# Router logits of three batches, one token tile at a time between the shared expert's matmuls, in a decoder layer

## The chip, the cores and the metric

The kernel runs on one core of one Trainium2 chip, as one program. The metric is the device time of one execution in microseconds (us); a time of the kernel is the median of several runs. One further execution is recorded by the hardware profiler, and all rows of a profile come from it.

A core has five engines that work through queues of their own and wait for each other through semaphores: PE (TensorE, matmuls and transposes), DVE (VectorE), ACT (ScalarE), POOL (GpSimd) and SP (SyncE, which here only issues DMAs). Matmuls write to PSUM[...]; everything else stands in SBUF or in DRAM.

## What is computed

One decoder layer on x of shape (4, 512, 512) in float32, with three parts, each on a layer norm of x and added to it:

```python
x = x + _L0_attn_ref(_layernorm(x), ...)     # a state space layer (conv, gate, scan)
x = x + _L0_xattn_ref(_layernorm(x), ctx_512, ctx_512)   # 32 query heads, 8 key heads of 16
x = x + _L0_ffn_ref(_layernorm(x), ...)      # mixture of experts
```

The last part is where the change lies. With x as 2048 tokens of 512:

```python
router_logits = x @ gate_w                       # 2048 x 16
scores = sigmoid(router_logits)
selected = top_k(scores + expert_bias, 2)
shared = silu(x @ shared_gate_w) * (x @ shared_up_w) @ shared_down_w
routed = sum over the two selected experts of weight * expert(x)
out = shared + routed
```

## The kernel before

Tokens stand 128 to a tile: NT = 16 tiles, TB = 4 tiles to each of B = 4 batches. The residual `res` stays in SBUF.

**Attention as the main loop.** After the state space layer of batch 0, the loop at L732 goes over 32 units (batch, key head) in 8 steps each. A step computes two score matmuls for the maxima of the next unit (`maxima`, pm, L496, with DVE's reduce L502), two for the weights of this unit (`weights`, pw, L513, with ACT's exponential L517), and in every second step `values` (pav, L522). Once a unit there are transposes: ptq and ptm of the queries (L484), ptv of the result (L531, `finish`). pm and pw alternate in the two buffers of the pool `p_sc`, so the pm of a step waits for the reduce of the step before it.

**Filler.** After each step `fill(step)` (L706) issues pieces of other work on PE: first the state space layers of batches 1 to 3, then `beside_last` (L668), the feed forward of batches 0 to 2. Such work is a generator that yields the us that a piece is thought to take; `fill` gives each step a quota, the total of the work over the steps left, and issues pieces until what is owed is paid, so after a long piece some steps get none. DVE and ACT work of the filler is put off by a step or more through `lag`. The orders on PE, DVE and ACT are as written; those of POOL and SP come from a scheduler. When the last filler begins, `open_ffn` (L546) opens its buffers and issues the loads of its weights on SP, fills a tile `zero` on POOL and stores it to the spare rows of h_d and of the output.

**The feed forward of one batch**, as filler:
- `ffn_first` (L587) normalizes the first two token tiles into `hn`, of which there are two buffers (tag "hn"). `zero` is a tile of the same tag.
- `ffn_input` (L591): for each of four tiles it stores hn to the DRAM copy h_d (L609), which the experts gather from later, transposes it (pth, L612), copies it to hT (ACT, L613) and normalizes the tile after next into the buffer set free. After the four tiles it computes the logits: `logits(j)`, four matmuls of 128x16 per tile (L601), one piece per tile, all into one PSUM tile pl, and then one copy to lgt (L622). With a bank_l given, as for batch 3 behind the main loop, the logits alternate with the transposes.
- `ffn_start` (L580) puts the norm statistics of the next batch (bnf, mvf, rstdf) into DVE's lagged work.
- `shared` (L624): for each of two halves f of the hidden size, pg and pu (L632, each four matmuls of 128x512, in two pieces), tanh on ACT (L640), two products on DVE (L643, L649); then pe (L655), one per token tile, added to res (L660) and stored to the output (L662).

In `beside_last` the next batch's statistics are begun after `ffn_input`, and `shared` runs on while they are made. PSUM tiles of all of these (pt.., pth, pl, pg, pu, pe) come from one pool of three banks (`bank`, tag "mm").

Behind the main loop come batch 3's feed forward input, the choice of experts from lgt (L840 on), and the loop over 47 blocks of tokens with gathered expert weights.

Of the kernel before, what the change touches and what calls it, by code (L numbers as in the profile page):

```python
# [10 lines left out]
F32 = mybir.dt.float32  # L11
# [6 lines left out]
P = 128  # L18
B, L, D = 4, 512, 512
NT = B * L // P  # L20
TB = L // P
# [10 lines left out]
E, F = 16, 256  # L32
# [13 lines left out]
def decoder_layer(ctx: ExitStack, tc: tile.TileContext, a: dict, out: bass.AP):  # L46
    nc = tc.nc
# [61 lines left out]
    def bank(name, shape=(P, L)):  # L109
        return p_mm.tile(list(shape), F32, tag="mm", name=name)  # L110
# [44 lines left out]
    def until(*tests):  # L155

        while not all(t() for t in tests):
            yield None
# [385 lines left out]
    ffn = {}  # L544

    def open_ffn():  # L546
        ssm_pools.close()
        hp_ = ctx.enter_context(tc.tile_pool(name="ffn_h", bufs=1, side="right"))
        ffn["hp"] = hp_
        ffn["hT"] = hp_.tile([P, DC, NT * P], F32, name="hT")  # L550
        ffn["lgt"] = hp_.tile([P, NT, E], F32, name="lgt")
        gw = ffn["gw"] = hp_.tile([P, DC, E], F32, name="gw")
        nc.sync.dma_start(out=gw, in_=a["gate_w"].rearrange("(c p) e -> p c e", p=P))
        ebias = ffn["ebias"] = hp_.tile([P, E], F32, name="ebias")
        nc.sync.dma_start(out=ebias, in_=a["expert_bias"].partition_broadcast(P))
        gu = ffn["gu"] = hp_.tile([P, DC, 2 * F], F32, name="gus")
        nc.sync.dma_start(
            out=gu[:, :, 0:F], in_=a["shared_gate_w"].rearrange("(c p) f -> p c f", p=P)
        )
        nc.sync.dma_start(  # L560
            out=gu[:, :, F:], in_=a["shared_up_w"].rearrange("(c p) f -> p c f", p=P)
        )
        zero = hp_.tile([P, D], F32, tag="hn", bufs=2, name="zero")
        nc.gpsimd.memset(zero, 0.0)
        for rows in (h_d, out):
            nc.sync.dma_start(out=rows[ts(NT, P), :], in_=zero)
        dn = ffn["dn"] = hp_.tile([P, FC, D], F32, name="dns")
        nc.sync.dma_start(out=dn, in_=a["shared_down_w"].rearrange("(c p) d -> p c d", p=P))
# [3 lines left out]
    def ffn_normed(b, j, eng):  # L572
        if j >= TB:
            return
        tt = b * TB + j
        hn = ffn["hp"].tile([P, D], F32, tag="hn", bufs=2, name=f"hn{tt}")
        normed(eng, hn, res[:, tt, :], *ffn["stats"], j)
        hns[tt] = hn

    def ffn_start(b):  # L580

        ffn["stats"], part, last = norm_parts(b, "f")
        return lag.add(
            *[(ENG.DVE, 0.9, lambda j=j: part(j)) for j in range(TB)], (ENG.DVE, 0.2, last)
        )

    def ffn_first(b, eng):  # L587
        for j in range(2):
            ffn_normed(b, j, eng)

    def ffn_input(b, bank, eng, bank_l=None):  # L591

        hp_, hT, lgt, gw = ffn["hp"], ffn["hT"], ffn["lgt"], ffn["gw"]
        pl = bank_l(f"pl{b}", (P, TB, E)) if bank_l else None

        def logits(j):
            nonlocal pl
            if pl is None:
                pl = bank(f"pl{b}", (P, TB, E))
            for c in range(DC):  # L600
                nc.tensor.matmul(  # L601
                    pl[:, j, :], lhsT=hT[:, c, ts(b * TB + j, P)], rhs=gw[:, c, :],
                    start=(c == 0), stop=(c == DC - 1),
                )

        for j in range(TB):
            tt = b * TB + j
            hn = hns.pop(tt)
            nc.sync.dma_start(out=h_d[ts(tt, P), :], in_=hn)  # L609
            pt = bank(f"pth{tt}", (P, DC, P))  # L610
            for c in range(DC):
                nc.tensor.transpose(pt[:, c, :], hn[:, ts(c, P)], ident)  # L612
            nc.scalar.copy(hT[:, :, ts(tt, P)], pt)  # L613
            ffn_normed(b, j + 2, eng)
            yield TR
            if bank_l and j > 0:
                logits(j - 1)
                yield 1.6
        for j in range(TB - 1 if bank_l else 0, TB):
            logits(j)  # L620
            yield 1.6
        nc.vector.tensor_copy(lgt[:, ts(b, TB), :], pl)  # L622

    def shared(t, bank):  # L624

        hp_, hT, gu, dn = ffn["hp"], ffn["hT"], ffn["gu"], ffn["dn"]
        act = hp_.tile([P, FC, L], F32, tag="act", bufs=2, name=f"act{t}")
        for f in range(FC):
            pg, pu = bank(f"pg{t}_{f}"), bank(f"pu{t}_{f}")
            for pp, lo in ((pg, f * P), (pu, F + f * P)):  # L630
                for c in range(DC):
                    nc.tensor.matmul(  # L632
                        pp, lhsT=gu[:, c, lo : lo + P], rhs=hT[:, c, ts(t, L)],
                        start=(c == 0), stop=(c == DC - 1),
                    )
                    if c == 1:
                        yield 2 * MM
                if pp is pg:
                    sg = hp_.tile([P, L], F32, tag="sg", bufs=2, name=f"sg{t}_{f}")
                    nc.scalar.activation(sg, pg, AF.Tanh, scale=0.5)  # L640
                    done = lag.add((
                        ENG.DVE, 0.75,
                        lambda sg=sg, pg=pg: nc.vector.scalar_tensor_tensor(  # L643
                            sg, sg, 1.0, pg, ALU.add, ALU.mult
                        ),
                    ))
                else:
                    yield from until(done)
                    nc.vector.tensor_mul(act[:, f, :], pu, sg)  # L649
                yield 2 * MM  # L650
        for j in range(TB):
            tt = t * TB + j
            po = bank(f"pe{tt}", (P, D))
            for f in range(FC):
                nc.tensor.matmul(  # L655
                    po, lhsT=act[:, f, ts(j, P)], rhs=dn[:, f, :],
                    start=(f == 0), stop=(f == FC - 1),
                )
            r = res[:, tt, :]
            nc.vector.scalar_tensor_tensor(r, po, 0.5, r, ALU.mult, ALU.add)  # L660

            nc.sync.dma_start(out=out[ts(tt, P), :], in_=r)  # L662
            yield 2 * MM

    SHARED_US = 6 * TB * MM
    FFN_US = TB * (TR + 1.6)

    def beside_last():  # L668
        ffn_first(0, nc.vector)
        for b in range(B - 1):  # L670
            yield from ffn_input(b, bank, nc.gpsimd)
            more = shared(b, bank)
            if b + 1 < B - 1:
                yield from until(lambda: finished >= KV * (b + 2))
                started = ffn_start(b + 1)
                while not started():
                    yield next(more)
                ffn_first(b + 1, nc.gpsimd)
            yield from more
# [20 lines left out]

    beside = [(lambda b=b: ssm(b), STEPS * (b * KV - 1) + 1, SSM_US) for b in range(1, B)]
    beside.append((beside_last, STEPS * (NU + 1), (B - 1) * (SHARED_US + FFN_US)))
    work, quota, owed = None, 0.0, 0.0
    finished = 0

    def fill(step):  # L706
        nonlocal work, quota, owed
        if work is None:
            if not beside:
                return  # L710
            make, until, us = beside.pop(0)
            if not beside:
                open_ffn()
            work = make()
            quota, owed = us / (until - step), 0.0
            fill.until = until
        owed += quota
        last = step >= fill.until - 1
        while owed > 0 or last:
            try:  # L720
                us = next(work)
            except StopIteration:
                work = None
                return
            if us is not None:
                owed -= us
            elif last:
                lag.step(dve=99.0)
            else:
                return  # L730

    for i in range(-1, NU):  # L732
# [5 lines left out]
        for s in range(STEPS):  # L738
# [9 lines left out]
            if i >= 0 and i + 2 < NU:  # L748
                b, v = units[i + 2]
# [36 lines left out]
    hT, lgt, ebias = ffn["hT"], ffn["lgt"], ffn["ebias"]  # L786
    with ExitStack() as ph:
# [252 lines left out]
        for _ in ffn_input(B - 1, bank_o, nc.vector, bank_g):  # L1040
            pass
# [94 lines left out]
```

## Time and profile before

| | |
|---|---|
| median of 3 runs (range) | 1618.39 us (1617.56 to 1618.58) |
| the profiled execution | 1618.54 us |
| its span, first to last instruction | 1616.8 us |
| mean granted clock of PE | 0.911 |
| PE waits for DVE's reduce (pm, L496), all steps | 17.8 us |
| PE waits for expert weights (L1003) | 42.3 us |
| logits, L601 | 128 rows of 128x16, 918.7 to 1219.6 us |
| copy of logits, L622 | 4 of 128x64, 0.215 us each |
| hn on DVE / on POOL (L97) | 0.546 us / 2.07 us each |

How to read it. A row of the timeline gives a start and a time from the start of the span in us, engine, line, operation, and output<-inputs by the program's names, with a count where rows were merged; what stands in brackets is the idle time of the engine before it and what ended that. A logical float32 matmul shows as two rows on PE, and PEld is the load of its weights. The granted clock is what PE's throttle lets through as a share of full speed. A view of stretches gives, for each, its length, the busy time of each engine with the number of instructions, the granted clock, and the share and rate of the DMA engines.

### The profile page before, as it was taken

How to read it: one execution, taken by the hardware profiler on the slowest of the kernel's cores; microseconds unless marked ns; L12 is line 12 of the kernel's file. 1: busy time of each engine (PE TensorE's matmuls, PEld its weight loads, DVE VectorE, ACT ScalarE, POOL GpSimd, SP SyncE). 2: the span in 40 equal slices, each digit the busy share in tenths (PEclk: the TensorE clock that was granted, in tenths of full speed). 3: DMA queues.
4: the chain of work that ended last, by engine and by line, in shares of the span. 5: the costliest groups of instructions: out<-in, count | busy, mean ns of one | idle time of the engine just before them, and what ended most of it. 6: DMA issues, size and time to landing. Idle time of an engine off the chain costs nothing. (4 is left out here: it accounts for less than half of the span.)

```text
span 1616.8 us, 15184 instructions
## 1 busy us (share of the span) xinstructions
PE 1472.6 (91%) x5922; PEld 579.8 (36%) x5922; DVE 693.8 (43%) x964; ACT 486.1 (30%) x646; POOL 360.3 (22%) x396
## 2 busy tenths in 40 slices
PE   6888999999999999999999799999978989888887
PEld 3333333333333333333333333333325534343433
DVE  5632566444556444466444344254326222222222
ACT  3210434422544333544433333344331111100110
POOL 4022400103201000310100211111000354544443
PEclk9988899988899999899989679598897899999998
DMA  8000000000000000000000200001012487889873
GB/s 311 21 1 0 0 4 5 6 4 4 4 13 4 4 6 5 4 4 7 4 4 5 81 18 32 17 20 43 1 39 101 120 268 193 260 272 293 255 202 53
DMA packets 36264, 108.67 MB, mean 67 GB/s; under 512 B 8096, under 2 KB 11296, under 8 KB 31456
## 3 DMA queue, kind: packets, MB, share of 16 engines
q0 software_dynamic: 17296, 79.71, 17.2%
q1 hardware_dynamic: 18032, 27.45, 5.1%
q8 instruction: 47, 0.77, 0.2%
q10 hardware_dynamic: 864, 0.55, 0.1%
q14 instruction: 25, 0.20, 0.0%
HBM read 105.31 MB, written 21.23 MB: 78 GB/s over the span
## 5 line engine op out<-in xcount | busy, mean ns | idle before, releaser
L502 DVE TENSOR_REDUCE qp<-pm 128x2 f32<-128x1024 f32 x256 | 313.6, 1225 | 439.0 <-PE pw L513 409.3
L517 ACT ACTIVATE ex<-pw 128x1024 f32<-128x1024 f32 x256 | 262.3, 1025 | 457.3 <-PE pw L513 449.4
L496 PE MATMUL pm<-kt,qTq 16*128 16x512 f32 x1024 | 314.4, 689 | 18.8 <-DVE qp L502 17.8
L513 PE MATMUL pw<-qTm,kt 17*128 17x512 f32 x1024 | 312.8, 688 | 0.1
L1003 PE MATMUL pgb<-wt,xT 128*128 128x512 f32 x376 | 184.3, 636 | 44.4 <-DMA wt<-in_experts,wrow_i 42.3
L97 POOL TENSOR_SCALAR qp<-res,mvq,rstdq 128x64 f32<-128x64 f32 x128 | 71.9, 578 | 501.1 <-PE ptm L484 411.4
L496 PEld LDWEIGHTS pm<-kt,qTq 16*128 16x128 f32 x1024 | 82.2, 195 | 193.4 <-issue 88.7
L522 PE MATMUL pav<-ex,va 128*32 128x512 f32 x1024 | 150.1, 661 | 0.1
L417 PE MATMUL po<-wout,zg 128*128 128x512 f32 x256 | 127.9, 635 | 0.0
L279 PE MATMUL px<-xnT,win 128*128 128x512 f32 x256 | 126.3, 630 | 0.0
L279 PE MATMUL pz<-xnT,win 128*128 128x512 f32 x256 | 121.8, 608 | 0.0
L1003 PEld LDWEIGHTS pgb<-wt,xT 128*128 128x128 f32 x376 | 72.6, 203 | 125.3 <-issue 121.0
L1010 DVE TENSOR_TENSOR actb<-pgb,sgb 128x256 f32<-128x256 f32 x47 | 20.0, 425 | 216.0 <-ACT sgb L1008 216.0
L541 POOL TENSOR_TENSOR res<-res,o 128x256 f32<-128x256 f32 x32 | 23.2, 725 | 326.5 <-DVE o L537 323.0
L1031 POOL DMA_INDIRECT out_x<-y,row_i x47 | 75.1, 1599 | 85.3 <-issue 50.5
L1025 PE MATMUL pob<-wt,aT 128*128 128x512 f32 x188 | 88.6, 593 | 0.5 <-ACT aT L1018 0.5
L513 PEld LDWEIGHTS pw<-qTm,kt 17*128 17x128 f32 x1024 | 81.5, 194 | 8.8 <-ACT ex L517 5.6
L1008 ACT ACTIVATE sgb<-pgb 128x256 f32<-128x256 f32 x47 | 18.1, 385 | 210.8 <-PE pgb L1003 210.8
L417 PEld LDWEIGHTS po<-wout,zg 128*128 128x128 f32 x256 | 47.1, 199 | 77.2 <-issue 74.2
L337 DVE SCALAR_TENSOR_TENSOR xc<-px,wcv,xc 128x511 f32<-128x511 f32 (+2 forms) x96 | 71.7, 747 | 5.7 <-ACT xc L333 3.5
L279 PEld LDWEIGHTS px<-xnT,win 128*128 128x128 f32 x256 | 47.1, 197 | 75.3 <-issue 75.0
L279 PEld LDWEIGHTS pz<-xnT,win 128*128 128x128 f32 x256 | 44.9, 189 | 69.3 <-issue 69.3
(190 smaller groups left out, 1433.9 us busy)
## 6 DMA issues: line engine op xcount, KB each, us to landing
kt<-in_ctx_t SPq DMA_DIRECT2D x128, 32.0 KB, 1.7
h_d<-hn SPq DMA_DIRECT2D x16, 256.0 KB, 2.1
out_x<-res SPq DMA_DIRECT2D x16, 256.0 KB, 2.0
res<-in_x SPq DMA_DIRECT2D x3, 1024.0 KB, 14.9
win<-in_w_in SPq DMA_DIRECT2D x2, 1024.0 KB, 9.6
wout<-in_w_out SPq DMA_DIRECT2D x1, 2048.0 KB, 14.1
win<-in_w_in SPq DMA_DIRECT2D x6, 256.0 KB, 7.0
win<-in_w_in SPq DMA_DIRECT2D x3, 512.0 KB, 6.7
```

What stands on the lines that cost most here:

```text
L97: eng.tensor_scalar(dst, src, mv[:, j, 0:1], rstd[:, j : j + 1], ALU.subtract, ALU.mult)
L279: nc.tensor.matmul(pm, lhsT=win[:, piece, c, :], rhs=xnT[:, c, :], start=(c == 0), stop=(c == DC - 1),)
L337: nc.vector.scalar_tensor_tensor(xc[:, d:], px[:, : L - d], wcv[:, i, KW - 1 - d : KW - d], xc[:, d:], ALU.mult, ALU.add,)
L417: nc.tensor.matmul(po, lhsT=zg[:, i, ts(j, P)], rhs=wout[:, i, :], start=(i == 0), stop=(i == IC - 1),)
L496: nc.tensor.matmul(ps[:, g - g0, :], lhsT=qT[g * SL : g * SL + HD, ts(j, P)], rhs=kts[i % NQ][g * SL : g * SL + HD, :], start=True, stop=True,
L502: nc.vector.tensor_reduce(qps[i % NQ][:, j, g0 : g0 + 2, HD], ps, AX.X, ALU.max, negate=True)
L513: nc.tensor.matmul(ps[:, g - g0, :], lhsT=kts[i % NQ][rows, ts(c, P)], rhs=qT[rows, :], start=True, stop=True,)
L517: nc.scalar.activation(ex[:, g0 : g0 + 2, :], ps, AF.Exp, scale=1.0 / HD**0.5)
L522: nc.tensor.matmul(pav[ts(g, SL), :], lhsT=vas[b % 2][:, c, v, :], rhs=ex[:, g, :], start=(c == 0), stop=(c == TB - 1),)
L1003: nc.tensor.matmul(pg, lhsT=xT[:, c, :], rhs=wts[k % NW][:, ts(c, 2 * F)], start=(c == 0), stop=(c == DC - 1),)
L1025: nc.tensor.matmul(po, lhsT=aT[:, f, :], rhs=wts[k % NW][:, lo : lo + D], start=(f == 0), stop=(f == FC - 1),)
L1031: nc.gpsimd.indirect_dma_start(out=out, out_offset=bass.IndirectOffsetOnAxis(ap=row_i[:, k : k + 1], axis=0), in_=y, in_offset=None, bound ...
```

## The change

The logits leave `ffn_input` when no bank_l is given. It leaves behind a list `ffn["logits"]` of four functions, one for each token tile; each takes a bank of its own, computes the four matmuls of its tile and copies 16 columns to lgt. `spread` wraps the generator of `shared` and, at every second piece of it, issues one of these functions ahead of the yield and adds its 1.6 us to the piece. The total that `fill` spreads over the steps is the same. Batch 3 goes as before. Apart from that `zero` becomes a tile of the tag "sg" (the tanh of the shared expert, also two buffers of the same size) and no longer one of "hn".

```diff
-        zero = hp_.tile([P, D], F32, tag="hn", bufs=2, name="zero")
+        zero = hp_.tile([P, D], F32, tag="sg", bufs=2, name="zero")
...
-        def logits(j):
-            nonlocal pl
-            if pl is None:
-                pl = bank(f"pl{b}", (P, TB, E))
+        def logits(j, at=None):
             for c in range(DC):
                 nc.tensor.matmul(
-                    pl[:, j, :], lhsT=hT[:, c, ts(b * TB + j, P)], rhs=gw[:, c, :],
+                    pl[:, j if at is None else at, :], lhsT=hT[:, c, ts(b * TB + j, P)], rhs=gw[:, c, :],
                     start=(c == 0), stop=(c == DC - 1),
                 )
...
-        for j in range(TB - 1 if bank_l else 0, TB):
-            logits(j)
+        def alone(j):
+            nonlocal pl
+            pl = bank(f"pl{b}_{j}", (P, 1, E))
+            logits(j, 0)
+            nc.vector.tensor_copy(lgt[:, b * TB + j, :], pl[:, 0, :])
+
+        if bank_l:
+            logits(TB - 1)
             yield 1.6
-        nc.vector.tensor_copy(lgt[:, ts(b, TB), :], pl)
+            nc.vector.tensor_copy(lgt[:, ts(b, TB), :], pl)
+        else:
+
+            ffn["logits"] = [lambda j=j: alone(j) for j in range(TB)]
...
+    def spread(work):
+        for n, us in enumerate(work):
+            if n % 2 == 1 and ffn["logits"]:
+                ffn["logits"].pop(0)()
+                us += 1.6
+            yield us
+
     def beside_last():
         ffn_first(0, nc.vector)
         for b in range(B - 1):
             yield from ffn_input(b, bank, nc.gpsimd)
-            more = shared(b, bank)
+            more = spread(shared(b, bank))
```

In the order of PE's instructions that results, the pieces of pg stand in the steps where the first two pieces of logits stood; each later logits tile follows the second piece of a pg or a pu. The statistics of batches 1 and 2 move forward by some steps with the end of `ffn_input`.

## The prediction

> **What bounds the kernel now.** I read the page's busy shares and clock row first, then the stretch that the change touches.
>
> ```profile
> PE 1472.6 (91%) x5922; PEld 579.8 (36%) x5922; DVE 693.8 (43%) x964; ACT 486.1 (30%) x646; POOL 360.3 (22%) x396
> PEclk9988899988899999899989679598897899999998
> ```
>
> TensorE (PE) is the bound, and its granted clock (tenths) sags most in the 23rd, 24th and 26th of the 40.4 us slices (6, 7 and 5), all in the stretch where attention of the last batch runs beside the router and the shared expert. I cut that stretch at its clock changes (columns: length, busy time of PE, PEld, DVE, ACT, POOL, then the granted clock):
>
> ```profile
> 901.33:942.29 40.96, 33.86 (x140) 15.80 (x144) 11.59 (x17) 13.02 (x16) 10.85 (x14) 0.50 0.24 80
> 973.01:1010.56 37.55, 33.58 (x182) 11.56 (x184) 18.81 (x21) 14.70 (x17) 5.94 (x10) 1.00 0.09 33
> 1010.56:1037.86 27.30, 26.87 (x116) 11.23 (x116) 6.13 (x5) 8.57 (x12) 6.37 (x6) 0.50 0.07 25
> 1123.20:1140.26 17.06, 17.06 (x64) 6.70 (x60) 5.03 (x5) 4.10 (x4) 0.00 (x0) 0.50 0.00 1
> ```
>
> The clock is full or half, and each half-clock stretch is a whole number of 3.41 us windows: 12, 8 and 5 here, and 1, 1, 1, 2 and 2 between (from 949.1, 959.4, 969.6, 1044.7, 1164.2), 32 in all, 109.2 us, with PE busy for 101.2 us of them. The three long ones are the places where the logits of batches 0, 1 and 2 run. The PE timeline shows what runs there:
>
> ```profile
> 914.81 1.22 PE L496 MATMUL pm<-kt,qTq 16*128 16x512 f32 x2
> ...
> 918.69 1.89 PE L601 MATMUL pl<-gw,hT 128*128 128x16 f32 x8
> ...
> 942.85 1.98 PE L632 MATMUL pg<-hT,gus 128*128 128x512 f32 x4
> ...
> 949.45 2.77 PE L632 MATMUL pg<-hT,gus 128*128 128x512 f32 x3
> ...
> 1010.30 1.01 PE L496 MATMUL pm<-kt,qTq 16*128 16x512 f32 x2 [1.31 <-DVE qp L502]
> ```
>
> From 914.8 to 942.3 PE has no gap, yet the clock stays at half. Cutting the whole trace into such windows, I find a sum that sorts 472 of 473 of them (an estimate, fitted to this trace): per us of full-rate work count 1 for a 128-row matmul with 512 columns (pg, pu, pe, po) and for pav, 0.9 for a transpose, 0.6 for pm with pw, 0 for logits; the next window has the full clock if the sum is 1.43 or more. At half clock a window holds only 1.71 us of full-rate work, so score steps (0.6) and logits (0) cannot bring the clock back, and 512-column matmuls can. The last line shows how it is lost: a step without filler waits 1.3 us for VectorE.
>
> **The sum of the old stretch.** I count from pm of step 0 at 895.32 to the pm at 1174.05: 71 steps, 278.7 us. Full-rate durations come from the starts: pm with pw 1.04, pav 1.0 (x34), four transposes 0.53 (x37), half of a pg, pu, pe or po (four rows of the trace) 1.91 (x32), logits of one token tile 0.92 (x12): 199.6 us. PE's waits:
>
> ```profile
> PE pm L496 <- DVE qp L502: 17.2, 20, 1.3
> PE pth L612 <- DVE hn L97: 7.2, 2, 4.4
> PE pth L612 <- POOL hn L97: 2.0, 4, 0.9
> PE ptv L531 <- ACT av L773: 0.7, 1, 0.7
> ```
>
> 27.1 us. The half clock costs 101.2 / 2 = 50.6, which is 1.58 per window. Together 277.3; 1.4 stays unexplained and is carried on.
>
> **Zero rows in another buffer.** It removes the wait of hn 1:
>
> ```profile
> 907.57 0.55 DVE L97 TENSOR_SCALAR hn<-res,mvf,rstdf 128x512 f32<-128x512 f32 x1 [5.00 <-DMA out_x<-zero]
> ...
> 909.58 4.13 POOL L97 TENSOR_SCALAR hn<-res,mvf,rstdf 128x512 f32<-128x512 f32 x2 [8.98 <-DMA h_d<-hn]
> ```
>
> hn 1 then ends at about 903.2 instead of 908.1, and its transposes and pm 2 run early. But hn 2 reuses hn 0's buffer, and its line says that it starts at 909.58, when hn 0's own store lands. That store is issued at 902.59 either way, behind the same weight loads. So the transposes of hn 2 stay at 911.7 and those of hn 3 at 913.8: PE waits 4.4 us there instead. The bounds are 0 and -4.4 us (if the store landed early); I take 0. The memset and the two stores are the same; the sg tile that inherits the zero rows' buffer is wanted tens of us later, and the stores land in 6.4 us.
>
> **Logits between the shared matmuls.** No matmul is added: the twelve logits tiles stay twelve. Copies out of PSUM become twelve 128x16 instead of three 128x64 (0.215 us each): at most 12 x 0.215 - 0.65 = 1.9 us of VectorE, and nothing if a copy of 16 columns costs a quarter of one of 64. Each copy waits for logits that stand on PE ahead of the next pm, so the reduce queued behind it, and the PE step that waits for that reduce, could not have started; I take 0. Of the three PSUM banks pg and pu hold two while a pl takes the third, which ptq, ptm and ptv want too; its copy follows in the same step, and the old pl held a bank from 918.7 to 944.3, so this is 0 as well (a bank late by a copy: 0.2 us each, 2.5 in all). The filler's budget per step is unchanged, but it now comes in lumps (a half and a logits tile together), so more steps are bare. A bare step lasts 2.45 us (pm to pm, VectorE's reduce between), which leaves PE idle 1.41 us with nothing else, 0.88 with a transpose, 0.41 with pav, 0.49 with logits only. Old order: 8, 6, 5 and 5 of these, 21.1 us, of which the trace shows 17.2 (half clock fills some). New order: 11, 9, 8 and 0, 26.7, and by the same ratio 21.8: +4.6 us.
>
> Statistics of batch 1's rows move about six steps forward, into the step that also has batch 3's query statistics. VectorE then has 1.23 + 0.87 + 0.2 + 0.87 + 0.2 = 3.4 us, ScalarE 1.02 + 1.28 + 0.30 + 1.28 + 0.60 = 4.5, PE 1.04 + 1.91 + 0.92 = 3.9; I take +0.6 (0 to 2). On POOL hn 4 and hn 5 (2 x 2.07) go ahead of an update of res and the next queries, which are wanted a unit later; on SP batch 2's two stores move ahead of four key loads that wait for PE anyway (they spread from 1028 to 1063). Both 0; without that cover up to 2 us each.
>
> One half of pu (1.9 us) that stood after the stretch now stands within it, so the old stretch to compare with is 280.6.
>
> **The clock is the main term.** The windows that I expect:
> - Batch 0: the same drop at 901.3. The first pg half now stands at 918.69, where the logits stood; at half clock it fills window 918.4 to 921.8 (0.92 us per row, from 2.77 for three). Full clock from 921.8: 6 windows instead of 12.
> - Batch 1: the drop before it is as likely as before; the first pg comes after the pav at 1022.5, so the clock is back at about 1027.6. 5 windows if it drops, none if not: I take 3 instead of 8.
> - Batch 2: bare and logits steps are broken up by pg and pu: 2 instead of 5.
> - Single drops: the old order drops 5 times at about 9 bare steps, 7 windows. The new one has 11 bare steps, three right behind logits, which count nothing, and two in a row: 6 drops, and as the next filler is further away, 2.2 windows each: 13 instead of 7.
>
> 24 windows instead of 32. New stretch: 201.5 + 9.9 + 21.8 + 0.6 + 1.4 + 24 x 1.58 = 273.1, against 280.6: 7.5 us less. The profiled execution takes 1618.54 us (span 1616.8), the median of the runs is 1618.39, so the difference goes over unchanged: 1611 us.
>
> [...] The row 1010.56:1037.86 (26.87 of 27.30 us busy, clock 0.50) decides: being busy is not what counts here.
>
> **The rivals.**
> - Slower: bare steps take the clock. Place: the second half of each shared expert, where after a lump two steps in a row have no 512-column matmul. Price 1.58 us a window. It decides from 45.4 / 1.58 = 29 windows on (280.6 - 235.2 = 45.4). At 36 the time is 1630. For it: 32 steps without any filler against 21, and old bare steps did drop the clock. Against it: the old three long runs were 25 windows by themselves. 0.20.
> - No change: the long runs shorten, single drops give it back, 27 to 31 windows, 1616 to 1622, middle 1618. For it: where a window begins relative to a step is chance, and only whole windows count. 0.20.
> - Faster, as summed: 0.60. Its own range is 17 to 26 windows, 1600 to 1615. If hn 0's store lands early as well, 4 us more.
>
> **Numbers.** About 0.2%, 3.2 us, is what a measurement of this kernel can tell from no change. The range 1600 to 1624 reaches from 17 windows into the slower rival as far as 32; left out are about 0.07 below and 0.11 above. Faster 0.60, same 0.20, slower 0.20.
>
> **What would show it.** The profile after should have the clock back near 921.8 (not 942.3) and no half-clock run over 6 windows after it; a wait of hn 2 for h_d<-hn still ending near 909.6 while hn 1's 5.0 us is gone; PE's wait for VectorE's reduce near 22 us instead of 17. I am wrong if half-clock windows from 895 to the end of the stretch number 29 or more, if the logits' 16-column matmuls do hold the clock, or if PE waits on copies or on keys that the trace of before does not show.

## The result, and the profile after

The changed kernel takes 1624.45 us (median of 20 runs, 1613.94 to 1630.50), the kernel before 1618.59 us on the same chip (20 runs, 1610.03 to 1623.77). The ratio is 1.0033, with a 95% interval of 1.0018 to 1.0049: slower, by about 5 us, where 7.5 us less had been forecast. The profiled execution of the changed kernel takes 1627.55 us (span 1625.8 us).

PE's busy time and the clock row of the page after:

```profile
PE 1475.7 (91%) x5922; PEld 579.0 (36%) x5922; DVE 695.2 (43%) x973; ACT 485.5 (30%) x646; POOL 361.4 (22%) x396
...
PEclk9978899989999989899989797779797899999999
```

PE issues the same 5922 matmuls. The deep dips of before (6 and 5) are gone; instead the seven slices of the stretch, the 23rd to the 29th, show 7, 9, 7, 7, 7, 9, 7. It is cut at its clock changes again, and these are five of its twelve half-clock runs (length, busy time of PE, PEld, DVE, ACT, POOL, the clock, DMA):

```profile
903.70:924.20 20.50, 13.18 (x44) 5.41 (x44) 5.49 (x10) 4.39 (x6) 4.13 (x2) 0.50 0.44 154
971.90:992.40 20.50, 19.18 (x63) 6.28 (x60) 5.78 (x6) 4.10 (x4) 0.00 (x0) 0.50 0.00 0
1009.50:1026.60 17.10, 16.66 (x60) 5.61 (x52) 3.68 (x3) 5.32 (x7) 4.13 (x2) 0.50 0.08 31
1053.90:1064.10 10.20, 10.06 (x32) 3.15 (x32) 2.54 (x3) 2.52 (x3) 0.00 (x0) 0.50 0.02 6
1135.80:1146.00 10.20, 10.15 (x32) 2.93 (x36) 3.04 (x3) 2.05 (x2) 0.00 (x0) 0.50 0.00 0
```

The first and the third are what is left of the long runs of batches 0 and 1: 6 windows of 3.41 us instead of 12, 5 instead of 8. The last is batch 2's: 3 instead of 5. So the three places that the change was expected to shorten had 25 windows and have 14. But the second and the fourth stand where the kernel before had one window or the full clock. With seven more (from 934.4, 1043.6, 1074.3, 1094.8, 1152.8, 1166.5 and 1176.7) they make nine drops with 20 windows, where before had five with 7. In all 34 windows instead of 32.

PE's waits in the stretch of the changed kernel (us in all, times, longest):

```profile
PE pm L496 <- DVE qp L502: 22.2, 25, 1.3
PE pth L609 <- POOL hn L97: 6.7, 4, 5.2
PE pth L609 <- DVE hn L97: 2.8, 1, 2.8
PE pg L638 <- ACT hT L610: 0.7, 1, 0.7
```

The reduce has 22.2 us instead of 17.2. The waits for hn have 9.5 instead of 9.2, for the most part with POOL as the releaser and no longer DVE. The timeline shows that hn 1 now follows hn 0 at once, and that hn 2 still waits for hn 0's store, 9.08 us:

```profile
904.23 1.00 DVE L97 TENSOR_SCALAR hn<-res,mvf,rstdf 128x512 f32<-128x512 f32 x2
...
911.91 4.13 POOL L97 TENSOR_SCALAR hn<-res,mvf,rstdf 128x512 f32<-128x512 f32 x2 [9.08 <-DMA h_d<-hn]
```

From pm of step 0 to the last pm, cut in the same way at both ends, the stretch lasts 288.3 us against 279.3.

### The profile page after: what moved, and what is told of

It is laid out like the page before. It is cut to its first block, busy times and chain, and to the rows that moved or that the text cites. A ratio compares the mean times of both kernels' runs of the same rounds, so it can differ in the third digit from the quotient of the medians.

```text
span 1625.8 us, 15196 instructions
## 1 busy us (share of the span) xinstructions
PE 1475.7 (91%) x5922; PEld 579.0 (36%) x5922; DVE 695.2 (43%) x973; ACT 485.5 (30%) x646; POOL 361.4 (22%) x396
```

## The experiments

**Theory.** The stretch lasts as long as its full-rate work and its waits, plus 1.58 us for each half-clock window. The change takes windows from the long runs and gives them to single drops, because filler now comes in larger lumps with a logits tile behind each, and the steps behind a lump have nothing that counts. **Rival.** The loss lies elsewhere: the waits for VectorE that grew, the twelve copies, or the zero rows, and the windows only go along with it.

The fourteen profiled executions, repeats among them, in the stretch from the first pm to the last. "Rest" is the length less a flat 1.58 us per window, good to some 3 us, since PE is not equally busy in all windows. "First drop" is the time from pm of step 0 to the first half-clock window of the stretch:

| kernel | first drop, us | windows | stretch, us | rest, us | median of all runs, us |
|---|---|---|---|---|---|
| before | 6.0 | 32 | 279.3 | 228.7 | 1618.59 |
| before, second execution | 8.9 | 33 | 282.2 | 230.1 | |
| zero rows alone | 8.9 | 33 | 282.2 | 230.1 | 1616.34 |
| after | 6.1 | 34 | 288.3 | 234.6 | 1624.45 |
| after, second execution | 6.1 | 32 | 284.9 | 234.3 | |
| after, logits as pieces of their own | 8.9 | 20 | 265.9 | 234.3 | 1604.18 |
| after, small pieces | 6.1 | 18 | 256.5 | 228.1 | 1598.00 |
| after, idle 128x512 matmuls | 8.8 | 7 | 251.3 | 240.2 | 1586.34 |
| before, idle 128x512 matmuls | 6.1 | 18 | 266.6 | 238.2 | 1603.86 |
| after, idle 128x16 matmuls | 6.1 | 31 | 284.3 | 235.3 | 1603.17 |
| the same, second execution | 8.8 | 23 | 276.1 | 239.8 | |
| before, zero rows and four hn buffers | 8.8 | 23 | 262.1 | 225.8 | 1600.21 |
| after, small pieces, own logits, four hn | 8.8 | 11 | 238.0 | 220.6 | 1580.02 |
| after, small pieces, idle matmuls, four hn | 6.1 | 4 | 229.0 | 222.7 | 1569.86 |

The first drop comes at two times only, 6.0 to 6.1 us and 8.8 to 8.9 us. So the program falls into one of two positions against the windows. The two executions of the kernel before differ in it, and so do the two with idle 128x16 matmuls, whose window counts differ as well (31 and 23). Window counts of single executions are therefore safest to compare within one position; where two rows differ in it, the medians over all runs have to carry the reading.

### The two kernels once more

No edit; one profiled execution each, to see how far the windows are chance.

> The changed kernel as it is, one more look. Theory (the time is the sum of 235 us of full-rate work and waits in the stretch and 1.58 us per half-clock window; where windows fall relative to steps is chance): the profiled time follows its own window count, 1618 us at 28 windows, 1627 at 34, 1634 at 38, while PE's wait for the reduce stays near 22 us. Rival (the loss has another cause that the windows only accompany): window count and time part by more than 4 us.

> The kernel before as it is, one more look. The same as for the changed kernel: about 28 to 35 windows, 1.58 us each around 1618.5 us at 32, so 1612 us at 28 and 1623 at 35. The long run in batch 0 (12 windows) should be there again, since its steps hold no 512-column matmul; rival: it is chance too and can be shorter.

After came at 1615.84 us with 32 windows, before at 1618.21 with 33. In the stretch the account holds: 284.9 and 282.2 us, and the rests (234.3, 230.1) stay within 1.4 us of those of the first execution. For the whole time of after it doesn't: 3.4 us less than the first execution's 1627.55 would be 1624, and it took 1616, so windows and time part by 8 us where the rival had set 4. The windows outside the stretch explain most of that. Over the whole span the first execution has 85.6 windows' length of half clock, the second 80.4: 5.2 x 1.58 = 8.2 of the 11.7 us between them. So one execution says little about a few us, and the stretch must be compared with itself. The long runs are the same in both executions (after: 6, 6, 5 and 3 again; before: 11 instead of 12, then 8 and 5 again). For before, whose executions differ in the first drop, the pattern belongs to the order of the work. For after this is not shown: both executions have the first drop at 6.1, and the pattern from the other position is not on record.

### The zero rows alone

```diff
-        zero = hp_.tile([P, D], F32, tag="hn", bufs=2, name="zero")
+        zero = hp_.tile([P, D], F32, tag="sg", bufs=2, name="zero")
```

> Only the zero rows' buffer is changed in the kernel of before. Clock theory and bare-step theory alike: 0 (1617 to 1620 us), since hn 2 still waits until about 909.6 for the store of hn 0, so the wait of hn 1 (5.0 us) only moves to hn 2's transposes. Rival, that the stall really goes: 4.4 us faster, 1614.

Ratio 0.9995 (0.9979 to 1.0011), which leaves at most some 3 us either way. Its waits are

```profile
PE pm L496 <- DVE qp L502: 17.2, 20, 1.3
PE pth L612 <- POOL hn L97: 7.9, 4, 6.3
PE pth L612 <- DVE hn L97: 2.8, 1, 2.8
```

Before, PE had two waits for DVE's hn, 2.8 us and 4.4 (hn 1). The second is gone, and hn 2 on POOL takes it over with 6.3. This part shows neither gain nor loss, and the loss lies with the logits.

### A logits tile as a piece of its own

The changed kernel, but the tile is no longer added to the piece ahead of it; it is charged and issued on its own, mostly a step later.

```diff
         for n, us in enumerate(work):
+            yield us
             if n % 2 == 1 and ffn["logits"]:
                 ffn["logits"].pop(0)()
-                us += 1.6
-            yield us
+                yield 1.6
```

> The changed kernel with each logits tile as a filler piece of its own, issued after the pg or pu half has been paid for, so that it falls into the next step: 21 steps without filler instead of 32, the 512-column matmuls in the same steps as in the changed kernel. Theory that the lump is what failed (a logits tile, which counts 0, always right behind the only 512-column matmuls, then empty steps): windows from 34 to about 24 to 28 and 5 us fewer waits of PE, 1608 to 1615 us. Rival, that only the places of the 512-column matmuls count: 32 to 36 windows, only the waits change, about 1619 us.

Ratio 0.9901 (0.9864 to 0.9938): 1604.2 us, with 20 windows instead of 34 and 17.8 us of waits for the reduce instead of 22.2. The longest runs are 5 windows (batch 0) and 3. That is more than was expected (24 to 28 windows, 1608 to 1615 us). The first drop is at the other position here, so the 14 windows may owe something to that; the medians, 6 runs against 20, do not hang on one execution, and only the slowest of the six (1614.75) is not faster than the fastest of the twenty (1613.94). Logits, copies, banks and order of the tiles are those of the change; only the lump is gone, and the time falls by 20 us, to below the kernel before. The rival of the copies and banks falls with it. What made the change slower is that the tile is issued with the piece ahead of it, its 1.6 us added to that piece, instead of being placed by `fill`.

### Small pieces

The changed kernel with the shared expert's work in pieces of one 128x512 matmul instead of two; the logits still ride on every fourth piece.

```diff
-                    if c == 1:
-                        yield 2 * MM
+                    if c < DC - 1:
+                        yield MM
...
-            if n % 2 == 1 and ffn["logits"]:
+            if n % 4 == 3 and ffn["logits"]:
```

The other yields follow suit, and behind the main loop `some(5)` and `some(4)` become 10 and 8.

> The changed kernel with the shared expert's pieces half as long: one 128x512 matmul to a piece instead of two, so 14 of 71 steps have no filler instead of 32. Clock theory (the changed kernel has 34 half-clock windows where 24 were summed, because its lumps leave steps without a 512-column matmul): at most about 12 to 18 windows, 25 to 35 us for the clock and some 8 us for PE's waits less than the changed kernel, 1582 to 1595 us. Rival, that the waits of PE for VectorE in bare steps are the whole cost and the clock is a bystander: only the waits, 1616 us.

Ratio 0.9863 (0.9833 to 0.9893), 18 windows, 13.4 us of waits for the reduce. Its first drop is that of the changed kernel (6.1), so here the 16 windows less can be read from the executions themselves. Steps without any filler fall from 32 to 14. The window count is the one expected, the time (1598) a few us above.

### Idle matmuls of 512 columns

In each step that got no dense filler (pth, pg, pu or pe) and has no pav, one 128x512 matmul more, whose result nobody reads. It adds work and leaves nothing out. Once on the changed kernel (20 steps), once on the kernel before (22 steps). Left out below: `dense[0]` is set where dense filler is issued.

```diff
+            dense[0] = False
             fill(step)
+            if "gu" in ffn and i + 1 < NU and not dense[0] and s in (0, 1, 2, 4, 6):
+                nc.tensor.matmul(
+                    bank(f"keep{step}"), lhsT=ffn["gu"][:, 0, 0:P], rhs=ffn["gu"][:, 0, :],
+                    start=True, stop=True,
+                )
```

> The changed kernel plus one idle 128x512 matmul (0.96 us at full clock, result never read) in each of 20 steps of the last batch's attention that have neither filler with 512 columns nor pav. Clock theory: half-clock windows in the stretch fall from 34 to 12 or fewer, 30 us or more less, about 1590 us, although PE does 19 us more work. Rival (bare steps' waits or the added copies are the cost): the added work fills waits and gains nothing, 1624 to 1630 us.

> The kernel of before with the same idle 128x512 matmuls in its 22 such steps. Clock theory: 32 half-clock windows fall to about 12, first of all the runs of 12 and 8, and the time to about 1590 us, no worse than the changed kernel with them: the two orders then differ by little. Rival: no gain, 1618 to 1625 us.

On the changed kernel: ratio 0.9807 (0.9783 to 0.9832), 1586.3 us, although PE has 20 matmuls more to do. All that is left of half clock in the stretch are these two runs, and the wait for the reduce falls to 5.5 us, since the idle matmul stands in it:

```profile
901.40:918.50 17.10, 9.80 (x35) 3.33 (x28) 4.01 (x6) 3.60 (x5) 4.13 (x2) 0.50 0.39 144
1000.40:1007.20 6.80, 6.27 (x22) 2.26 (x23) 1.23 (x1) 1.61 (x2) 0.47 (x1) 0.50 0.11 39
```

The rest column goes up by 5.6 us (240.2), the 27 windows less give 42.7 back. Nothing was taken from the kernel: a bare step at full clock lasts 2.46 us with the idle matmul as without it (step 10 in both traces), so what goes is half clock, and the time follows it. All five runs (1583.5 to 1590.9 us) lie below the fastest of the changed kernel, so this does not hang on where the windows fall.

On the kernel before: 0.9916 (0.9893 to 0.9940), 1603.9 us and 18 windows, where about 1590 and 12 were expected. All its single drops are gone and so is batch 2's run of 5, but the runs of batches 0 and 1, which were to go first, stay:

```profile
902.40:946.80 44.40, 37.49 (x144) 16.66 (x148) 11.53 (x17) 13.00 (x16) 10.88 (x14) 0.50 0.22 74
1018.50:1035.60 17.10, 17.10 (x70) 7.09 (x66) 3.68 (x3) 4.13 (x5) 2.00 (x4) 0.50 0.04 10
```

Idle matmuls stand in these runs too (at 925.2, 935.5 and 1027.1), one at a time between logits and score matmuls, and the clock doesn't come back: at half clock one of them holds 2.05 us for its 0.96 us of full-rate work (half of the prediction's 1.91), and by the sum of the prediction, an estimate, what shares the window with it counts little, so it stays below the bar. A single dense matmul in a step with a wait held the clock (the single drops, 7 windows, are gone), but one at a time did not win it back. In batch 0 of the changed kernel it came back at 924.2, near the end of two dense matmuls in a row (pg from 921.03, 3.52 us); the kernel before has no such pair there (12 windows, here 13).

### Idle matmuls of 16 columns

The same 20 steps, with four 128x16 matmuls (the shape of a logits tile) in place of one of 128x512.

```diff
+                kp = bank(f"keep{step}", (P, E))
+                for c in range(DC):
+                    nc.tensor.matmul(
+                        kp, lhsT=ffn["gu"][:, c, 0:P], rhs=ffn["gu"][:, c, 0:E],
+                        start=(c == 0), stop=(c == DC - 1),
+                    )
```

> The changed kernel with the same 20 steps filled, but by four idle 128x16 matmuls (about 0.92 us at full clock, like one logits tile) instead of one 128x512. The sum of the prediction counts such matmuls as 0: half-clock windows in the stretch stay at about 34 (30 to 40), and the added work costs something where the clock is half: 1624 to 1640 us. Rival, that PE only has to be without gaps for the clock: as with the 128x512 matmul, about 7 windows and 1586 us.

> The changed kernel with four idle 128x16 matmuls in the 20 steps without dense filler, one more look. Its profiled run was at 1618.7 us with 31 windows, most other runs at 1602. If 16-column matmuls count a little (0.13 per us), a run near 1602 us has about 20 windows. Rival (they count nothing and 1602 has another cause): about 31 windows whatever the time.

Ratio 0.9903 (0.9870 to 0.9937), 1603.2 us: neither the 1624 to 1640 of work that counts nothing nor the 1586 of the rival. They fill PE's waits as well as the others do (4.5 us left of 22.2). The profiled execution took 1618.70 us with 31 windows, against 34 of the changed kernel from the same first drop (6.1); but of the other five runs four took 1601 to 1603. The second execution, at 1608.39 us, has 23 windows from the other first drop, where 512 columns left 7. So 16 columns are far from what 512 do, compared at that same first drop. Whether the 21 us come from 16 columns counting a little, which tips some windows and not others, or in part from where the windows fall, stays open.

### Four buffers for hn

The kernel before with the zero rows in "sg" and four hn buffers.

```diff
-        hn = ffn["hp"].tile([P, D], F32, tag="hn", bufs=2, name=f"hn{tt}")
+        hn = ffn["hp"].tile([P, D], F32, tag="hn", bufs=4, name=f"hn{tt}")
```

> The kernel of before with the zero rows in the other buffer and four buffers for hn instead of two. If hn 2's wait for the store of hn 0 took the place of hn 1's wait, this one takes both away: pm 3 about 6.6 us earlier, 5 to 7 us faster than before, 1612 us. Rival, that the start is bound by something else (clock, statistics on VectorE): 0 to 2 us.

Ratio 0.9884 (0.9851 to 0.9917), 18 us less. The expectation was too small by the clock: the rest falls by 4 us against the zero rows alone (6, if the windows are priced by PE's busy time in them), as the waits for POOL's hn go, but 10 windows go as well (33 to 23). Most of these are batch 1's run of 8 (steps 27 to 32), which does not come at all. Here are steps 27 to 33, with the same logits tiles in the same places, at full clock:

```profile
1009.90:1029.90 20.00, 19.35 (x148) 9.77 (x148) 9.27 (x9) 11.02 (x15) 2.98 (x5) 1.00 0.03 8
```

The same work kept half clock for 27.3 us in the kernel before (the row 1010.56:1037.86 of the prediction). So logits among score steps, pav and transposes kept a full clock for these 20.0 us (it drops at 1030.1, behind the last tile, for 3 windows), but did not win one back in those 27.3, and the 8 windows hang on the one drop ahead of them. That the drop is gone because the waits moved the steps against the windows is argued, not shown.

### Together

The changed kernel with small pieces and four hn buffers, once with idle 128x512 matmuls in the steps that still have nothing (8 of them are left), once without, but with each logits tile as a piece of its own.

```diff
-            if n % 2 == 1 and ffn["logits"]:
-                ffn["logits"].pop(0)()
-                us += 1.6
             yield us
+            if n % 4 == 3 and ffn["logits"]:
+                ffn["logits"].pop(0)()
+                yield 1.6
```

> The changed kernel with half-size pieces, the idle 128x512 matmul in the 8 bare steps still left to it, and four hn buffers. Clock theory: half-clock windows 7 or fewer, PE's added work only 8 us, waits as in the half-size run: 1575 to 1585 us, faster than either part alone. Rival, that half-size pieces and idle matmuls reach the same limit: 1586 us as with the idle matmuls alone.

> The changed kernel with three edits and no matmul added: the filler in pieces of one 128x512 matmul, each logits tile a piece of its own, four hn buffers. Clock theory (what decides is how many steps in a row have no dense matmul): only 5 steps are left without any filler, so about 12 to 18 half-clock windows in the stretch and PE waits for VectorE's reduce of about 13 us; with the waits for hn gone too, 1578 to 1590 us. Rival (the gain of the version with idle matmuls came from those, and order alone cannot give it): no better than the four hn buffers alone or the fine pieces alone, 1596 to 1602 us.

With the idle matmuls: 0.9686 (0.9660 to 0.9713), 1569.9 us, 4 windows, the fastest here, 49 us below the kernel before and some 5 below the expected range. Without: 0.9745 (0.9713 to 0.9777), 1580.0 us, 11 windows, 9.1 us of waits for the reduce. That is within the expected time, and better than either edit alone, so order and buffers alone, with no work added, give four fifths of it (38.6 of 48.7 us). In its clock row one of the slices from the 23rd to the 29th shows 7, where after has five:

```profile
PEclk9988899989999999999998979999977999999999
```

## Why the prediction was wrong

**The terms that held.** PE is busy for 104.9 us of the 34 half-clock windows, which cost half of that, 52.4. The stretch without them is 235.9 us; forecast were 235.2. Its parts held too: waits for the reduce 21.8 forecast, 22.2 measured; hn and the other waits 9.9 against 10.2; zero rows 0, measured 0.9995; copies and banks 0, and no wait for a logits copy or a bank appears in PE's waits. The long runs held: batch 0 came back to the full clock 20.5 us after it dropped, as forecast (6 windows), batch 1 had the 5 windows of the case that it drops, batch 2 had 3 for 2. And the sum over windows held: with 34 of them it gives 235.2 + 34 x 1.58 = 288.9, and 288.3 was measured.

**The step that failed** is the line "6 drops, and as the next filler is further away, 2.2 windows each: 13 instead of 7". Nine drops came, with 20 windows, and nine again in the second execution (18 windows). Six of the nine follow a bare step (971.9, 1043.6, 1053.9, 1074.3, 1166.5, 1176.7). That number was right, but they hold 16 windows, 6 of them in the one run from 971.9. The other three (934.4, 1094.8, 1152.8; 4 windows) follow steps whose only other work is the transpose ptq, and these were left out: I had counted bare steps and carried over how often those had dropped before. That makes seven of the ten windows by which the forecast fell short; two are batch 1's (5, where the chance of none had made it 3), one is batch 2's. Here is how a window falls short behind a lump, in batch 2 (the shared matmuls ahead, the logits tile, the score matmuls after it and the next shared ones; rows of pw left out):

```profile
1130.68 1.98 PE L638 MATMUL pg<-hT,gus 128*128 128x512 f32 x4
...
1132.50 0.96 PE L598 MATMUL pl<-gw,hT 128*128 128x16 f32 x8
1133.39 0.70 PE L496 MATMUL pm<-kt,qTq 16*128 16x512 f32 x2
...
1135.85 1.22 PE L496 MATMUL pm<-kt,qTq 16*128 16x512 f32 x2 [1.31 <-DVE qp L502]
...
1141.75 3.78 PE L638 MATMUL pu<-hT,gus 128*128 128x512 f32 x4
```

The window from 1132.4 to 1135.8 holds the last 0.1 us of pg, a logits tile that counts 0 and one step of pm with pw: by the prediction's own weights 0.1 + 0.6 x 1.04 = 0.7, where 1.43 are wanted. By that sum, an estimate, the time that a logits tile fills is as good as idle for the clock, so the next step without dense work drops it: four drops of the twelve (1053.9, 1074.3, 1135.8, 1152.8) stand behind such a step right after a logits tile. Laid over the trace of after, the sum misses two windows of the stretch clearly (below); a few more lie within 0.1 of the bar. Laid over the new order ahead of the run, in place of a scaled count, it might have shown seven of the nine drops; where the windows would fall was not known then, so this is not shown.

**The cause of the longest new run** is the same. At 971.9 the clock drops behind a bare step, and the next lump comes 1.5 us later:

```profile
973.37 3.78 PE L638 MATMUL pu<-hT,gus 128*128 128x512 f32 x4
...
976.95 1.73 PE L598 MATMUL pl<-gw,hT 128*128 128x16 f32 x8
...
989.79 3.27 PE L661 MATMUL pe<-dns,act 128*128 128x512 f32 x4
```

The window boundary at 975.3 cuts it. By the sum the first window gets 0.97 of pu and some 0.44 of score matmuls, 1.41; the second gets 0.82 and then logits. Neither reaches 1.43, if the first only just, and the next shared matmul is 13 us away: 6 windows. The boundary fell there again in the second execution (971.1, 6 windows), which has the same position against the windows. What the other position would make of this lump is not on record. In both executions a lump of 1.9 us with no dense matmul close on either side was cut so and did not bring the clock back.

**A mis-sized term.** The two windows that the sum misses (934.4 and 1094.8, both one window long) stand behind steps of pm, pw and a transpose. Fitted over all fourteen profiles, the weights are 0.46 for pm with pw (0.6 forecast), 0.24 for one of them alone, 0.85 for a transpose (0.9), 0.13 for logits (0) and 1.38 for the bar (1.43); so set, the sum sorts more than 98 in 100 windows. This is an estimate that fits these traces; its weights move by up to 0.1 with how the time of overlapping rows is shared out, its bar does not. It accounts for two of the ten windows (3 of 16 us).

**The rivals.** The slower one came true by its mechanism: past 29 windows, behind lumps, at steps without a 512-column matmul. Its place was too narrow: four of the nine drops (971.9, 1074.3, 1166.5, 1176.7) stand in the second half of a shared expert, the others do not. It had 0.20, because the old order's 25 windows in long runs looked like more than single drops could give back. They took 13 where 11 were saved. That being busy is not what counts, as the prediction read from the kernel before, held: 16 columns and 512 keep PE busy in the same steps (4.5 and 5.5 us of waits for the reduce are left), but 16 left 31 and 23 windows where 512 left 7. And PE stood at half clock while busy for 17.10 of 17.10 us (the row 1018.50:1035.60).

What stays open is how often the boundary falls well, and why the first drop has two positions. In 20 runs the changed kernel spread over 16.6 us, and only two of its executions are profiled.

## What to carry to other kernels

Where the traces show a clock that goes with how dense the matmuls of a short window are (here 3.41 us), lay the windows over the new order as well as the old, step by step; a count scaled from the old order misses the new weak steps, and a window count from one execution holds for one position of the windows (31 and 23 here for one kernel). Give a scheduler small pieces and let each be placed by itself: a cheap piece glued to a costly one leaves holes, and here that was worth 20 us. Where a hole could not be filled, one wide matmul whose result nobody reads cost less here than the clock that the hole lost (20 of them took 38 us off), but it held a clock and did not win one back (runs of 13 and 5 windows stayed in the kernel before).

## What the runs showed of the hardware

- PE at half clock with no gap stayed at half clock over score matmuls, logits, pav, transposes and one idle matmul: 17.10 us busy of 17.10, clock 0.50, over 1018.50:1035.60 of the kernel before with idle matmuls. At full clock logits among score steps kept it for 20 us: clock 1.00 over 1009.90:1029.90 of the kernel with four hn buffers. By the fit over the fourteen profiles, an estimate, a window counts as full from 1.38 of its 3.41 us of dense full-rate work (40%); at half clock it holds at most 1.71, so by the fit four fifths of it have to be dense for the clock to come back.
- Twenty idle matmuls of 128x512, about 1 us each at full clock as filler in waits of up to 1.3 us, took 38 us off; eighty of 128x16 in the same steps took 21 in the median, and in one execution 6.
- The window boundaries lie 0.2 us (before) and 2.5 us (after) past a whole number of windows from the span's start. Yet in the fourteen profiled executions the first drop of the stretch came at one of two times (6.0 to 6.1 or 8.8 to 8.9 us after pm of step 0).
- The same kernel had 85.6 and 80.4 windows' length of half clock over its span in two executions (1627.6 and 1615.8 us), and another 31 and 23 windows in the stretch (1618.7 and 1608.4 us).
